# Pairwise field products: two stores split by partitions, ScalarE issuing the later stores, GpSimd giving TensorE's turns

## The chip, the cores and the metric

The kernel runs on one core of a Trainium2 chip. The metric is the device time of an execution in microseconds (us); the time before is the median of three runs. An execution's span, from its first to its last instruction, stands in the profile beside it.

## What is computed

The reference takes x of 4096 samples x 32 fields x 64 values, and a matrix W of 64 x 64, all float32:

```
vid = jnp.einsum('bfd,de->bfe', x, W)
idx_i, idx_j = jnp.triu_indices(32, k=1)
return x[:, idx_i, :] * vid[:, idx_j, :]
```

For each pair of fields i < j (496 pairs) the output is field i of x times field j of x times W, value by value. The output has 4096 x 496 x 64 float32 values, 520 MB; x has 33.6 MB.

## The kernel before

*Layout.* Two halves of the batch lie side by side in the 128 partitions (2 x 64 values), and the batch is cut into 16 tiles of 128 samples a half. One "field" of a tile is 128 partitions x 128 float32 values, 512 bytes a partition. `mem` in SBUF holds 446 such fields: inputs and products share it. On the HBM side a partition's fields lie one behind the other, in x as in the output, so that each DMA takes one contiguous run from each partition. The weights stand twice on the diagonal of a 128 x 128 matrix, so one matmul serves both halves.

*Work.* For each tile TensorE multiplies four fields at a time (line 237; 8 matmuls a tile) into `vid`, which fills PSUM. VectorE (line 173) makes the 496 products of a tile, many pairs an instruction, from `mem` and `vid` into `mem`. 68 stores ("slots") bring the products out, in the order in which they are made. `SLOTS` gives each store's number of fields and its place in `mem`; the places are reused again and again.

*Loads.* Tiles 0 to 5 are loaded at the start, by ScalarE's DMA queue. The other inputs come in two stretches of two loads each (128 and 32 fields): `LOAD_BEHIND = [24, 45]` says that SyncE issues them behind 24 and 45 stores. Stores are numbered from 0, so these are the places behind stores 23 and 44, of 128 fields each. Behind each stretch `held` makes the issuing engine wait, ahead of its next store, until the first matmul on the newly loaded tile (tile 6, tile 11) is done.

*Queues.* The class `Queue` wraps an issuing engine: `after_products(n)` waits until VectorE has done n instructions (line 133), `after(s)` waits for a DMA's semaphore to reach 16, each of them at most once. SyncE (`sp`) issues stores 0 to 65 (line 304) and the two stretches (line 198); ScalarE (`act`) issues the first loads and the last two stores. A DMA's semaphore gets 16 when all of it has landed.

*Turns.* TensorE waits for the semaphore `go` twice a tile (line 236 takes it back). ScalarE gives these turns: it waits until the half tile's fields have landed and VectorE has read the PSUM banks for the last time, and then increments `go`.

*The end.* ScalarE waits for all stores but the last and clears the semaphores; SyncE waits for the last store.

Of the kernel before, what the change touches and what calls it, by code (L numbers as in the profile page):

```python
# [12 lines left out]
P = 128  # L13
# [5 lines left out]
BANK = 4  # L19
# [33 lines left out]
LOAD_BEHIND = [24, 45]  # L53


SP_SLOTS = len(SLOTS) - 2

PAD = 24
PAD0 = 8
# [19 lines left out]
def products(at, ends):  # L79


    for kind, a, b, c, d in by_block():
        if kind == "row":
            rows, n, i0, di, j0, dj = c, d, b, 0, a, 1
        else:
            rows, n, i0, di, j0, dj = 16 // b, c, a, b, a + c + d, b
        r = k = 0
        while r < rows:
            room = ends[bisect_right(ends, at)] - at
            if k or room < n:  # L90
                m, w = 1, min(n - k, room)
            else:
                m, w = min(rows - r, room // n), n
            yield at, m, w, i0 + r * di + k, di, j0 + r * dj, dj
            at += m * w
            if k + w == n:
                r, k = r + m, 0
            else:
                k += w


HALF = F // 2


def fields(tiles, lo, n):

    return [(t, u - PLACE[t]) for u in range(lo, lo + n) for t in tiles if 0 <= u - PLACE[t] < F]
# [16 lines left out]
class Queue:  # L124
# [8 lines left out]
            self.engine.wait_ge(self.dve, n)  # L133
            self.products = n

    def after(self, s, known_to_product=None):

        if s.num not in self.seen and not (known_to_product and known_to_product <= self.products):
            self.engine.wait_ge(s, 16)
        self.seen.add(s.num)  # L140


# [33 lines left out]
def build(nc, x0, x, w, out):  # L176
    mem = nc.alloc_sbuf_tensor("mem", [P, UNITS, C], F32).ap()
    w2 = nc.alloc_sbuf_tensor("w2", [P, P], F32).ap()
    vid = nc.alloc_psum_tensor("vid", [P, F, C], F32).ap()

    go = nc.alloc_semaphore("go")
    pe = nc.alloc_semaphore("pe")
    dve = nc.alloc_semaphore("dve")
    sems = [go, pe, dve]

    def sem(name):
        sems.append(nc.alloc_semaphore(name))
        return sems[-1]

    track = Track()  # L190
    loaded = {}
    stored = []

    sp, act = Queue(nc.sync, dve), Queue(nc.scalar, dve)

    def load(q, dst, src, name, fields):
        s = sem(name)
        q.engine.dma_start(dst, src).then_inc(s, 16)
        for t, f in fields:
            loaded[t, f] = s  # L200
        return s


    a = PLACE[0]
    load(act, mem[:, a : a + HALF, :], x0[:, :HALF, :], "x0", [(0, f) for f in range(HALF)])
    ws = load(act, w2, w, "w", [])

    at = 0
    first_read = {}

    def stretch(q, tiles, runs, name):
        nonlocal at
        made = []
        for r, (lo, n) in enumerate(runs):
            q.after_products(track.reads(lo, lo + n))
            for k in track.stores(lo, lo + n):
                q.after(stored[k], first_read.get(k))
            made.append(load(q, mem[:, lo : lo + n, :], x[:, at : at + n, :], f"{name}{r}", fields(tiles, lo, n)))
            for u in range(lo, lo + n):
                track.store[u] = None  # L220
                track.read[u] = 0
            at += n
        return made

    held = stretch(act, *HEAD, "h")[-2], 16

    for tiles, first, step in WALKS:
        with nc.tensor.Fori(0, len(tiles)) as k:
            for b in range(F // BANK):
                if b % (HALF // BANK) == 0:
                    nc.tensor.wait_ge(go, 1)
                    nc.tensor.sem_inc(go, -1)  # L236
                nc.tensor.matmul(  # L237
                    vid[:, b * BANK : b * BANK + BANK, :],
                    lhsT=w2,
                    rhs=mem[:, bass.ds(k * step + (first + b * BANK), BANK), :],  # L240
                    start=True,
                    stop=True,
                ).then_inc(pe, 1)


    ends = sorted({*STARTS, *(STARTS[k] + c for k, cuts in CUTS.items() for c in cuts)})
    vector = Products(nc.vector, dve)
    done = 0
    bank_read = [0] * (F // BANK)
    dve_pe = dve_dve = 0  # L250
    slot = 0
    waiting = list(LOAD_BEHIND)
    stretches = list(STRETCHES)

    for t in range(NT):
        place = PLACE[t]
        for b in range(0, F // BANK, HALF // BANK):
            for s in [ws, *(loaded[t, f] for f in range(b * BANK, b * BANK + HALF))]:
                act.after(s)
            act.after_products(max(bank_read[b : b + HALF // BANK]))  # L260
            nc.scalar.sem_inc(go, 1)

        xt = mem[:, place : place + F, :]
        start = done
        for pos, m, n, i, di, j, dj in products(t * NP, ends):
            begin = STARTS[slot]
            size, lo = SLOTS[slot]
            u = lo + pos - begin
            o = mem[:, u : u + m * n, :]
            if m == 1:  # L270
                left = xt[:, i : i + n, :]
                right = vid[:, j : j + 1, :].to_broadcast([P, n, C])
            else:
                o = o.rearrange("p (m w) c -> p m w c", m=m)
                right = vid[:, j : j + (m - 1) * dj + 1 : dj, :].unsqueeze(2).to_broadcast([P, m, n, C])
                if di == 0:
                    left = xt[:, i : i + n, :].unsqueeze(1).to_broadcast([P, m, n, C])
                else:
                    left = xt.rearrange("p (m d) c -> p m d c", d=di)[:, i // di : i // di + m, i % di : i % di + n, :]
            waits = {}  # L280
            need = t * (F // BANK) + (j + (m - 1) * dj) // BANK + 1
            if need > dve_pe:
                waits[pe] = dve_pe = need
            for s in track.stores(u, u + m * n):
                if s not in first_read:
                    waits[stored[s]] = 16
                    first_read[s] = done + 1
            if track.reads(u, u + m * n) > dve_dve:
                waits[dve] = dve_dve = track.reads(u, u + m * n)

            vector.add(waits, done if t == 0 else start if t in FRESH else 0, o, left, right)
            done += 1
            for r in range(m):
                for f in range(i + r * di, i + r * di + n):
                    track.read[place + f] = done
                bank_read[(j + r * dj) // BANK] = done
            if pos + m * n == begin + size:
                if held is not None:
                    nc.sync.wait_ge(*held)
                    held = None  # L300
                q = sp if slot < SP_SLOTS else act
                q.after_products(done)
                s = sem(f"s{slot}")
                q.engine.dma_start(out[:, begin : begin + size, :], mem[:, lo : lo + size, :]).then_inc(s, 16)  # L304
                stored.append(s)
                for u in range(lo, lo + size):
                    track.store[u] = slot
                slot += 1
                if waiting and waiting[0] == slot:
                    waiting.pop(0)  # L310
                    tiles, runs = stretches.pop(0)
                    stretch(sp, tiles, runs, f"g{slot}_")
                    held = pe, tiles[0] * (F // BANK) + 1
    vector.emit()


    *landed, final = stored
    for k, s in enumerate(landed):
        act.after(s, first_read.get(k))
    numbers = sorted(s.num for s in sems)  # L320
    assert numbers == list(range(numbers[0], numbers[-1] + 1)) and final.num == numbers[-1]
    nc.scalar.sem_clear(range(numbers[0], numbers[-1]))
    nc.sync.wait_ge(final, 16)
    nc.sync.sem_inc(final, -16)
# [41 lines left out]
```

## Time and profile before

| what | value |
|---|---|
| median of three runs | 1284.24 us (1284.15 to 1284.56) |
| the profiled execution | 1284.14 us |
| its span | 1282.6 us |
| VectorE busy | 1080.3 us, 292 instructions |
| TensorE busy | 179.8 us, 256 matmuls |
| GpSimd busy | 0.2 us, 4 instructions |
| moved by DMA | 553.73 MB, mean 432 GB/s |
| HBM read, written | 33.62 MB, 520.09 MB |

A few marks for reading the lines below. PE is TensorE, DVE VectorE, POOL GpSimd; SPq and ACTq are the sequencers of SyncE and ScalarE, which issue DMAs; L173 is line 173 of the kernel. A line on a DMA queue gives packets, MB, and the time that the packets took as a share of the 16 DMA engines' time in the window asked for. A packet is listed in the window in which it starts, with its whole time, so that short windows can show shares over 100%. A line of waits gives the total in us, the number of waits and the longest. A line of the table of windows gives the window, its length, the busy time of PE, PEld, DVE and POOL (with counts), the granted clock, the DMA share, and GB/s. A line of the timeline or of the chain gives the start and the length in us.

### The profile page before, as it was taken

The page shows a single profiled execution, that of the slowest core. Times are in us where ns is not written, and L with a number is a line of the kernel's source. Part 1 is how long each engine was busy: PE and PEld are TensorE (multiplying, and loading weights), DVE is VectorE, ACT ScalarE, POOL GpSimd, SP SyncE. Part 2 cuts the span into 40 slices and gives each one's busy share as a digit, 9 for nine tenths or more (in the row PEclk, how much of TensorE's full clock was granted, in tenths as well). Part 3 has the DMA queues.
Part 4 walks back from the last instruction along what each step waited for, and adds up shares of the span by engine and source line. Part 5 has one row for each costly group of instructions (what it writes and reads, how often), then busy time and mean ns, then how long its engine had stood idle before and what let it go on. Part 6 is the DMA issues. An engine that isn't in the chain of part 4 may idle for free. (4 is left out here: it accounts for less than half of the span.)

```text
span 1282.6 us, 1142 instructions
## 1 busy us (share of the span) xinstructions
PE 179.8 (14%) x256; PEld 70.4 (5%) x256; DVE 1080.3 (84%) x292; POOL 0.2 (0%) x4
## 2 busy tenths in 40 slices
PE   3011040304010031012111201002212030111000
PEld 1000010101000010000000000001000010000000
DVE  5898999999996456989999998483898999899971
POOL 0000000000000000000000000000000000000000
PEclk7655565755565565565565656556557565565555
DMA  9999999999999999999999999999999999999999
GB/s 421 419 441 437 425 442 426 441 421 439 444 413 450 417 437 439 429 441 423 435 421 433 432 456 417 435 416 434 450 433 425 425 456 427 425 444 437 427 425 409
DMA packets 11090, 553.73 MB, mean 432 GB/s; under 512 B 1232, under 2 KB 1360, under 8 KB 1360
## 3 DMA queue, kind: packets, MB, share of 16 engines
q1 hardware_dynamic: 10080, 524.82, 94.7%
q10 hardware_dynamic: 1008, 28.90, 5.3%
q14 instruction: 2, 0.02, 0.0%
HBM read 33.62 MB, written 520.09 MB: 432 GB/s over the span
## 5 line engine op out<-in xcount | busy, mean ns | idle before, releaser
L173 DVE TENSOR_TENSOR mem<-mem,vid 128x1024 f32<-128x1024 f32 (+11 forms) x292 | 1080.3, 3770 | 174.8 <-DMA out_dram<-mem 144.4
L237 PE MATMUL vid<-mem,w 128*128 (+1 forms) x256 | 179.8, 870 | 1004.8 <-PEq L236 1004.8
L237 PEld LDWEIGHTS vid<-mem,w 128*128 128x128 f32 x256 | 70.4, 289 | 1113.4 <-issue 1113.4
L339 POOL MEMSET const-bfloat16-1.0<- 128x1 bf16 x1 | 0.1, 102 | 0.0
L339 POOL MEMSET const-uint8-127<- 128x1 uint8 x1 | 0.1, 102 | 0.0
L339 POOL MEMSET const-float32-0.0<- 128x1 f32 x1 | 0.1, 99 | 0.2 <-issue 0.2
L339 POOL MEMSET const-float32-1.0<- 128x1 f32 x1 | 0.1, 99 | 0.0
## 6 DMA issues: line engine op xcount, KB each, us to landing
out_dram<-mem SPq DMA_DIRECT2D x11, 7680.0 KB, 31.0
out_dram<-mem SPq DMA_DIRECT2D x11, 7168.0 KB, 23.1
out_dram<-mem SPq DMA_DIRECT2D x8, 6656.0 KB, 21.9
out_dram<-mem SPq DMA_DIRECT2D x4, 6144.0 KB, 24.2
out_dram<-mem SPq DMA_DIRECT2D x2, 5120.0 KB, 20.7
out_dram<-mem ACTq DMA_DIRECT2D x1, 7680.0 KB, 27.4
mem<-in_r_x_dram SPq DMA_DIRECT2D x2, 2048.0 KB, 60.5
out_dram<-mem SPq DMA_DIRECT2D x1, 3072.0 KB, 20.5
```

Source lines behind the costliest of these rows:

```text
L173: self.engine.tensor_tensor(*operands, MULT).then_inc(self.dve, 1)
L237: nc.tensor.matmul(vid[:, b * BANK : b * BANK + BANK, :], lhsT=w2, rhs=mem[:, bass.ds(k * step + (first + b * BANK), BANK), :], start=True ...
L339: nc = _bacc.Bacc("TRN2", target_bir_lowering=False, num_devices=1, dynamic_dma_scratch_size=256)
```

## The change

- Stores 23 and 44, the ones ahead of the two stretches of loads, are cut: 104 of the 128 fields go in one DMA of 128 partitions, and the last 24 fields in three DMAs, of partitions 0 to 111, 112 to 119 and 120 to 127. All four add to one semaphore, and whoever waits for the store waits for 64 instead of 16.
- Stores behind the second stretch (45 to 67) are issued by ScalarE, and so is the wait `held` ahead of them. Before, SyncE issued all but the last two.
- GpSimd gives TensorE's turns (`go`) instead of ScalarE.

```
-SP_SLOTS = len(SLOTS) - 2
+LATE = 24
+SPLIT = [0, 112, 120, 128]
...
-    sp, act = Queue(nc.sync, dve), Queue(nc.scalar, dve)
+    sp, act, gate = Queue(nc.sync, dve), Queue(nc.scalar, dve), Queue(nc.gpsimd, dve)
...
-                act.after(s)
-            act.after_products(max(bank_read[b : b + HALF // BANK]))
-            nc.scalar.sem_inc(go, 1)
+                gate.after(s)
+            gate.after_products(max(bank_read[b : b + HALF // BANK]))
+            nc.gpsimd.sem_inc(go, 1)
...
-                    waits[stored[s]] = 16
+                    waits.update([stored[s]])
...
+                q = sp if stretches else act
                 if held is not None:
-                    nc.sync.wait_ge(*held)
+                    q.engine.wait_ge(*held)
                     held = None
-                q = sp if slot < SP_SLOTS else act
                 q.after_products(done)
+                cut = size - LATE if slot + 1 in LOAD_BEHIND else size
+                parts = [(0, P, 0, cut)]
+                if cut < size:
+                    parts += [(p0, p1, cut, size) for p0, p1 in zip(SPLIT, SPLIT[1:])]
                 s = sem(f"s{slot}")
-                q.engine.dma_start(out[:, begin : begin + size, :], mem[:, lo : lo + size, :]).then_inc(s, 16)
-                stored.append(s)
+                for p0, p1, a, b in parts:
+                    q.engine.dma_start(
+                        out[p0:p1, begin + a : begin + b, :], mem[p0:p1, lo + a : lo + b, :]
+                    ).then_inc(s, 16)
+                stored.append((s, 16 * len(parts)))
```

More of the change, by code (lines that the diff above doesn't have):

```diff
@@ L134, in after_products, with after @@
             self.products = n
-    def after(self, s, known_to_product=None):
+    def after(self, s, n=16, known_to_product=None):
         if s.num not in self.seen and not (known_to_product and known_to_product <= self.products):
-            self.engine.wait_ge(s, 16)
+            self.engine.wait_ge(s, n)
         self.seen.add(s.num)
@@ L216, in stretch @@
             for k in track.stores(lo, lo + n):
-                q.after(stored[k], first_read.get(k))
+                q.after(*stored[k], first_read.get(k))
             made.append(load(q, mem[:, lo : lo + n, :], x[:, at : at + n, :], f"{name}{r}", fields(tiles, lo, n)))
@@ L314, in build @@
     vector.emit()
-    *landed, final = stored
-    for k, s in enumerate(landed):
-        act.after(s, first_read.get(k))
+    *landed, (final, _) = stored
+    for k, (s, n) in enumerate(landed):
+        act.after(s, n, first_read.get(k))
     numbers = sorted(s.num for s in sems)
```

## The prediction, made before the changed kernel was run

> **What bounds the kernel now.** I read the page's head first, then its DMA queues, then the waits, then single moments of the DMA list. The head, the DMA line and the queue part:
>
> ```profile
> span 1282.6 us, 1142 instructions
> PE 179.8 (14%) x256; PEld 70.4 (5%) x256; DVE 1080.3 (84%) x292; POOL 0.2 (0%) x4
> DMA  9999999999999999999999999999999999999999
> q1 hardware_dynamic: 10080, 524.82, 94.7%
> q10 hardware_dynamic: 1008, 28.90, 5.3%
> ```
>
> VectorE is the busiest compute engine, but the DMA line has a 9 in all 40 slices, and the two queues (q1 is fed by SyncE, q10 by ScalarE) take 94.7 + 5.3 = 100% of the 16 engines' span. Of VectorE's idle time, and of SyncE's, the waits say:
>
> ```profile
> DVE mem L173 <- DMA out_dram<-mem: 144.4, 31, 20.2
> DVE mem L173 <- PE vid L237: 30.3, 6, 11.5
> SPq L304 <- DVE mem L173: 1039.2, 62, 33.2
> SPq L198 <- DMA out_dram<-mem: 2.2, 2, 1.7
> ```
>
> VectorE waits 144.4 us for stores to free memory. SyncE waits for VectorE, yet this starves nothing, because a store once issued still stands in line. The table of windows shows the rate, and the summary of the stores (all instructions on the output) the time in line:
>
> ```profile
> 4.00:444.00 440.00, 68.31 (x96) 26.70 (x96) 388.89 (x105) 0.00 (x0) 0.58 1.00 434
> DMA to landing us min/median/max: 18.3/25.5/40.6
> ```
>
> The last column is GB/s. The queues move 524.82 + 28.90 = 553.72 MB, at 434 GB/s 1275.9 us. The span is 1282.6, so only 6.7 us of it are anything else: the start, the end, and what is lost at some moments. That is all a change of the transfers' order can win.
>
> Where is it lost? The DMA view of a short window lists the packets that start in it: their count, MB, and their time as a share of 16 engines in that window. So share x window = mean time of one round of 16 packets. Around the first stretch of loads (SyncE issues it behind store 23, and it moves about 447 to 472 us), one fence per window: 438.9 to 440 (middle of store 23), 443.9 to 445 (its last packets), 447.15 to 447.8 (first packets of the load, with 16 semaphore writes).
>
> ```profile
> q1 hardware_dynamic: 16, 1.05, 220.2%
> ```
> ```profile
> q1 hardware_dynamic: 16, 1.05, 285.1%
> ```
> ```profile
> q1 hardware_dynamic: 32, 1.05, 405.3%
> ```
>
> That is 2.202 x 1.1 = 2.422 us for a usual 65,536-byte packet, 2.851 x 1.1 = 3.136 us for the last of the store, 4.053 x 0.65 = 2.634 us for the first of the load. The change from store to load costs (3.136 - 2.422) + (2.634 - 2.422) = 0.93 us on every engine. The same before the second stretch, windows 841.6 to 842.6 and 844.6 to 845.4:
>
> ```profile
> q1 hardware_dynamic: 16, 1.05, 304.7%
> ```
> ```profile
> q1 hardware_dynamic: 32, 1.05, 323.0%
> ```
>
> 3.047 and 2.584 us: 0.62 + 0.16 = 0.79 us. Both together 1.72 us. From load back to store nothing is lost: 869.05 to 869.58, the first 57,344-byte packets of store 45:
>
> ```profile
> q1 hardware_dynamic: 32, 0.92, 400.9%
> ```
>
> 4.009 x 0.53 = 2.125 us for packet and semaphore write; 57,344/65,536 of 2.422 is 2.119.
>
> **The change, part by part.** The sum stands against the profiled execution, 1284.14 us (span 1282.6 and 1.5 around it); the median of the three runs is 1284.24, 0.1 above it.
>
> *Rows.* Stores 23 and 44 (128 fields each) become 104 fields for all 128 partitions, and 24 fields in three DMAs of 112, 8 and 8 partitions. No byte is added. In this trace a packet is one partition's row of a DMA: 128 rows give 16 engines 8 packets each, as the windows above show (16 equal packets at a time). A 24-field row is 12,288 bytes, 12,288/65,536 x 2.422 = 0.454 us. 112 rows are 7 for each of 16 engines. Where 8 rows go, no row here shows. Bounds: the two sets on different halves of the engines, 0; the same 8 engines twice, which then carry 9 rows instead of 8, +0.45 us a stretch, while the other 8 carry 7, -0.45; all on one engine, (7 + 16 - 8) x 0.454 = +6.8. I take the same eight: two DMAs of one shape go alike, as all the full ones do. **+0.91 us** for two stretches, on the half that sets the end.
>
> The Trainium skill's page "DMA: Bandwidth & Descriptors", section "Why a DMA increments its semaphore by 16 and not by 1", says that such a DMA uses the largest number of engines up to 16 that divides its outer size, and the lowest-numbered ones. By it 112 rows use 16 engines, and both sets of 8 the same first eight; the rows' term would be this +0.91 by the rule and 0 if the sets fell apart; no run here shows it.
>
> *More packets.* About 9 more data packets and 3 more semaphore writes on an engine a stretch. Small packets of the load, 470 to 471.6 us:
>
> ```profile
> q1 hardware_dynamic: 40, 0.66, 95.5%
> ```
>
> 0.955 x 1.6 x 16 / 40 = 0.611 us for 16,384 bytes; a quarter of 2.422 is 0.606. So 0.005 x 9 plus three writes under 0.01 each: at most 0.08 a stretch, **+0.1 us** in all.
>
> *The store-to-load loss.* Ends: none comes back (0), all comes back (-1.72). For the value I take engines that arrive late. Window 842.0 to 842.2, then 842.4 to 842.6, each hold one engine's last packet of store 44; the other 14 started before 841.95:
>
> ```profile
> q1 hardware_dynamic: 1, 0.07, 96.2%
> ```
> ```profile
> q1 hardware_dynamic: 1, 0.07, 81.0%
> ```
>
> 0.962 x 0.2 x 16 = 3.08 us and 0.81 x 0.2 x 16 = 2.59: the engine that is some 0.6 us late lost 0.17 against a mean of 0.62. The heavy half will come 0.9 us behind the light one, so it should lose some 0.45 less, and about 0.1 less on the load's first packet: **-1.1 us** over two stretches. The shorter packet in flight at the switch speaks for more, the light half's early reads for less.
>
> *The last engine.* The end is that of the slowest engine. Of the last semaphore writes, 1281.3 to 1281.65 and 1282.0 to 1282.2:
>
> ```profile
> q10 hardware_dynamic: 14, 0.00, 2.2%
> ```
> ```profile
> q10 hardware_dynamic: 1, 0.00, 0.3%
> ```
>
> One engine ends at least 0.35 us behind 14 others, at most 0.9. If it belongs to the light half the end comes earlier by about that, otherwise not. The halves' lead may be smaller by then, so I take less than the mean of the two: **-0.1**, ends -0.9 and 0.
>
> *Issues.* SyncE issues three DMAs more ahead of each stretch, 3 x 0.33 us:
>
> ```profile
> 408.16 0.33 SPq L304 DMA_DIRECT2D out_dram<-mem  x1
> 410.19 1.62 SPq L198 DMA_DIRECT2D mem<-in_r_x_dram  x2
> ```
> ```profile
> 809.43 0.33 SPq L304 DMA_DIRECT2D out_dram<-mem  x1
> 810.26 2.09 SPq L198 DMA_DIRECT2D mem<-in_r_x_dram  x2
> ```
>
> The first loads wait for a landed store until 410.19 anyway; the second ones go out some 0.5 us later. Their packets begin 34 us after the issue, at 844.6, behind stores in line; without that line it would cost 1.0 a stretch. So **0**. Semaphores of these two stores count to 64 instead of 16; VectorE's reuse waits see the same landing. Stores 45 to 67 go out from ScalarE with the same waits in the same order; behind them ScalarE has only the closing waits, and SyncE nothing but the last. The turns for TensorE, which would else stand behind these stores, move to GpSimd, which has 0.2 us of work.
>
> *The turn behind a load.* This is the one place with a thin cover. The chain, and ScalarE's first issue:
>
> ```profile
> 865.46 2.08 PE vid L237 x2
> 867.54 0.02 issue
> 867.56 0.34 SPq L304
> ```
> ```profile
> 0.72 0.38 ACTq L198 DMA_DIRECT2D mem<-in_r_x_dram  x1
> ```
>
> Store 45 is issued at 867.56, when the first matmul on the load is done. From issue to first packet takes 1.04 us (the DMA view has no packet up to 1.76 us and two at 1.76, after the issue at 0.72; the row is that of 0.5 to 1.77):
>
> ```profile
> q10 hardware_dynamic: 2, 0.02, 7.7%
> ```
>
> So its descriptors are there at about 868.60, and its first packet starts at 869.07 as the load ends: 0.47 us of cover. GpSimd's wait and increment aren't in the trace. Its only rows are four memsets like this:
>
> ```profile
> L339 POOL MEMSET const-float32-0.0<- 128x1 f32 x1 | 0.1, 99 | 0.2 <-issue 0.2
> ```
>
> Two such steps a turn would be 0.2 us; so I bound the turn at 0.2 us faster and 0.2 us slower than ScalarE's. I take **0**, covered by the 0.47. The light half may stand idle some tenths here, which its lead of 0.9 pays.
>
> Sum: +0.91 + 0.1 - 1.1 - 0.1 = -0.2: 1284.14 - 0.2 = 1283.9; with the median's 0.1, **1284.0 us**.
>
> **The rivals.**
>
> *No refund.* The heavy half carries its rows and loses as much at the switch as now: +0.91 + 0.1 = 1285.2 us. For it: the loss falls on all 16 engines, also on those a little late (3.08 us above). Against: the 2.59.
>
> *Full refund.* Small staggered packets switch from writing to reading without loss, and the sets fall on different halves, or the halves level out during the switch: -1.72 + 0.1 = 1282.5 us. For it: the loss is only in packets at the switch.
>
> *The turn comes late.* GpSimd answers a landed load so slowly that the DMA engines run dry: each stretch costs what the delay has above 0.47 us. It decides (0.2%, 2.6 us) from 0.47 + 1.3 = 1.8 us on; at 2.5 us it is 2 x 2.03 = +4.1, 1288.2 us. Against: landing to matmul now takes 0.4 us in all (the second load lands 54.8 us after its issue at 810.26):
>
> ```profile
> mem<-in_r_x_dram SPq DMA_DIRECT2D x1, 54.8
> ```
>
> *Each DMA pays a start of its own.* ScalarE's small load of the weights takes 4.8 us from issue to landing:
>
> ```profile
> w<-in_L_rec_W_dram ACTq DMA_DIRECT2D x1, 64.0 KB, 4.8
> ```
>
> If each of six more DMAs put even 2 us of that on the path, 1296 us. Against: the 434 GB/s above run over some two dozen DMAs in one queue. The same page of the Trainium skill, section "Anatomy of one DMA", gives a fixed 2.0 us a DMA, on another issuing path; it would make six DMAs 12 us; the trace disagrees for DMAs that stand in line.
>
> *One engine takes the eight rows twice:* +13.6 us, 1297.8. For it only that no row excludes it.
>
> **How the numbers follow.** Forecast (between 1283.2 and 1284.8) 0.55; no refund 0.17; full refund 0.17; late turn 0.05; a start for each 0.02; one engine 0.02; more than the whole loss saved 0.02 (1281.5 or less). From no change, 0.2% (2.6 us, 1281.7 to 1286.8) can be told. So faster 0.02 (the last case), slower 0.08 (0.04 of the late turn, whose other 0.01 stays within the bound, and 0.04 of the two dear ones), same 0.90. The range takes in both bounds of the switch and of the rows: 1282.4 to 1285.4; it leaves out the dear rivals and tails of the others.
>
> **What would show it.** In the changed trace: the last store packets before a load are 12,288 bytes and start in two groups some 0.9 us apart (rows right); packets at the switch sum to less than 0.93 and 0.79 us over their usual time (refund); store 45's first packet follows the load's last without a gap and stands on q10 (turn); the final semaphore writes come in one group rather than two (the halves level out). The prediction is wrong if the DMA share drops for over 1 us at 37% or 68% of the span, or if the final writes are spread over more than 2 us.

## The result, and the profile after

The changed kernel takes 1288.88 us (median of 6 runs, 1288.53 to 1289.11); the kernel before, run beside it, 1284.2. The ratio is 1.0035, 95% interval 1.0024 to 1.0045: slower by 4.7 us. The prediction had said 1284.0, within 1282.4 to 1285.4, and was wrong.

The head and the DMA lines of the changed kernel's profile:

```profile
span 1287.6 us, 1148 instructions
DMA  9999999999999999999999999999999999999999
DMA packets 11410, 553.74 MB, mean 430 GB/s; under 512 B 1296, under 2 KB 1424, under 8 KB 1424
```

The span grew by 5.0 us. The bytes (553.74 MB against 553.73) and the full DMA line are as before. So either the same bytes took longer *in their packets*, while the DMA engines still look busy, or the engines stood idle too briefly for the line. The page's slices, 32 us each, can't show which; the landing times of the loads show where. The DMA view of a short window lists the issues in it with the time to landing, in us, as the last number. First load of the first stretch before (issued at 410.19) and after (412.06), first load of the second stretch after (816.16):

```profile
mem<-in_r_x_dram SPq DMA_DIRECT2D x1, 57.6
```
```profile
mem<-in_r_x_dram SPq DMA_DIRECT2D x1, 58.3
```
```profile
mem<-in_r_x_dram SPq DMA_DIRECT2D x1, 54.2
```

Landed: 410.19 + 57.6 = 467.8 before, 412.06 + 58.3 = 470.4 after, +2.6. The second: 810.26 + 54.8 = 865.1 before, 816.16 + 54.2 = 870.4 after, +5.3. So each stretch adds about 2.6 us, and the two together are the whole loss.

Inside the switch, packets that start in 443.5 to 447 (93 of the last 24 fields, and a semaphore write), then 447.14 to 447.2 (two packets):

```profile
q1 hardware_dynamic: 94, 1.14, 99.5%
```
```profile
q1 hardware_dynamic: 2, 0.02, 426.4%
```

0.995 x 3.5 x 16 / 93 = 0.60 us a packet, and 4.264 x 0.06 x 16 / 2 = 2.05 us for those two; the price in the prediction was 0.454. Not all of the difference comes from the cut: over all 128 packets of the last 24 fields the mean is 0.65 us in this trace, and 0.55 where one DMA of all rows brings them to the same switch (`SPLIT = [0, 128]`, below). Then the table of windows, 472 to 473.6 (GB/s last, the DMA share before it), and the chain there:

```profile
472.00:473.60 1.60, 1.60 (x3) 0.57 (x3) 0.00 (x0) 0.00 (x0) 0.50 0.48 205
```
```profile
470.38 0.04 POOLq L264
...
470.73 2.08 PE vid L240 x2
...
472.83 19.32 DMA out_dram<-mem
```

At 205 GB/s about half of the engines stand dry, while the others still finish their loads: store 24 goes out only at 472.83 (before: 470.23), after the first matmul, which needs the load from the *slowest* engine. (The trace counts two instructions for each matmul of the program, 256 for 16 tiles of 8, hence "x2".) GpSimd itself is quick: landed at 470.35, matmul at 470.73.

### The profile page after: what moved, and what is told of

Its sections match the earlier page's. It is cut to its first block, busy times and chain, and to the rows that moved or that the text cites. A ratio compares the mean times of both kernels' runs of the same rounds, so it can differ in the third digit from the quotient of the medians.

```text
span 1287.6 us, 1148 instructions
## 1 busy us (share of the span) xinstructions
PE 182.3 (14%) x256; PEld 71.0 (6%) x256; DVE 1080.4 (84%) x292; POOL 0.2 (0%) x4
## 2 busy tenths in 40 slices
DMA packets 11410, 553.74 MB, mean 430 GB/s; under 512 B 1296, under 2 KB 1424, under 8 KB 1424
## 4 chain that ended last, share of the span: by engine, by line
DVE 34%; DMA 24%; another core or an unknown queue 16%; issue 1%; PE 1%; ACTq 0%; POOLq 0%; DVEq 0%
DVE mem L175 34%; DMA out_dram<-mem 24%; PE vid L240 1%; ACTq L312 0%; POOLq L264 0%; DVEq L173 0%
```

## The experiments

Each is a copy of the kernel before or of the changed one, with the edit shown. "Before" beside them took 1284.1 to 1284.3 us.

**The parts of the change, one at a time.** The cut alone:

```
-                q = sp if stretches else act
+                q = sp if slot < SP_SLOTS else act
...
-            nc.gpsimd.sem_inc(go, 1)
+            nc.scalar.sem_inc(go, 1)
```

> The cut of stores 23 and 44 alone; SyncE issues stores 0 to 65 and ScalarE gives the turns, as before. The changed kernel took +4.7 us. Theory A (crowding: the rows of the sets 112-119 and 120-127 lie behind few ports of SBUF, so that the engines that carry such a set share them; seen as 12,288-byte packets of 1.2 to 2.1 us where 0.46 is usual): all of it is here, 1288 to 1289.5. Theory B (the turns by GpSimd and the stores by ScalarE come late; SyncE issued store 24 at 472.83 instead of 470.23): 1284 to 1285.2, the row skew at most.

Measured 1289.54 us, ratio 1.0040 (1.0026 to 1.0055). The queues alone:

```
-                cut = size - LATE if slot + 1 in LOAD_BEHIND else size
+                cut = size
```

> ScalarE issues the stores behind the second stretch, GpSimd gives the turns, no store is cut. Theory A (crowded ports): 1284.2 within 0.6. Theory B (late turns and issues): 1288 to 1289.

Measured 1284.0, ratio 0.9997 (0.9988 to 1.0007). The whole loss is in the cut; who issues stores and who gives turns makes no difference that can be measured.

**Small packets, without other partitions.** `SPLIT = [0, 128]`, so the last 24 fields go in one DMA of all rows:

> Stores 23 and 44 as 104 fields and 24 fields, both of all 128 partitions, queues as before. Small packets at the switch, without a skew and with each engine on rows of its own. Theory A (crowded ports): 1283.3 to 1284.5. Theory C (it is the small packets ahead of a load that lose, each of them): 1287 to 1289. The prediction's idea that a shorter packet at the switch gets part of the 1.7 us back would show as 1282.5 to 1283.8.

Measured 1284.58, ratio 1.0002 (0.9992 to 1.0012). Small packets ahead of a load lose nothing that can be told, and get nothing back (1284.58 lies just above theory A's 1284.5).

**Halves against even and odd.** Both cut the 24 fields into two DMAs of 64 rows, 4 rows an engine each; they differ in which partitions go together:

```
 halves:        SPLIT = [0, 64, 128]
 even and odd:  SPLIT = [(0, 128, 2), (1, 128, 2)]   # first, end, step
```

> The last 24 fields by partitions 0-63 and 64-127: two DMAs that give each of 16 engines 4 rows, no skew, 8 packets of 12,288 bytes an engine as in the version of all rows. The Trainium skill's page SBUF - State Buffer, section Door 1, says that partitions 0-63 reach 8 of the 16 ports. Theory A (crowded ports): two engines share a port all through, 8 x 0.454 us become 8 x 0.91, +3.6 us a stretch, 1288 to 1291.5. Theory C (small packets) and theory D (skew of the halves, which then wait for the slowest at the load): as the version of all rows, 1283.3 to 1284.7.

> The last 24 fields of stores 23 and 44 by the even and the odd partitions: like the version of halves two DMAs of 64 rows, 4 rows an engine each, no skew, 8 packets of 12,288 bytes; only which partitions are read together differs, and here each DMA reaches all 16 ports. Theory A (crowded ports): engines still meet on a port, but can step apart; 1285 to 1289.5, at least 2.5 us under the halves (1292.2). If 64 rows in a DMA cost by themselves, whatever the partitions: 1291.5 to 1293.

Halves: 1292.22, ratio 1.0061 (1.0044 to 1.0078). Even and odd: 1284.77, ratio 1.0005 (0.9995 to 1.0015). The contrast is that of theory A, but both lie outside its ranges: halves 0.7 us above 1291.5, even and odd 0.2 us below 1285, with no loss that can be told. The table of windows, 443.2 to 445.2, for halves, even and odd, and all rows in turn:

```profile
443.20:445.20 2.00, 0.00 (x0) 0.00 (x0) 0.00 (x0) 0.00 (x0) 0.50 1.02 233
```
```profile
443.20:445.20 2.00, 0.00 (x0) 0.00 (x0) 0.07 (x1) 0.00 (x0) 0.50 1.06 449
```
```profile
443.20:445.20 2.00, 0.00 (x0) 0.00 (x0) 0.24 (x1) 0.00 (x0) 0.50 1.00 424
```

All three have a DMA share of 1.0, but halves move 233 GB/s and the others 449 and 424. Of the packets that start in 444.2 to 445.2, again for halves, even and odd (11 of the 46 are semaphore writes), and all rows:

```profile
q1 hardware_dynamic: 18, 0.22, 107.5%
```
```profile
q1 hardware_dynamic: 46, 0.43, 101.7%
```
```profile
q1 hardware_dynamic: 32, 0.39, 92.7%
```

1.075 x 1 x 16 / 18 = 0.96 us a packet with halves, 0.46 with the other two: a factor of two. Halves and even and odd have the same rows a DMA, the same packets and no skew: only the partitions differ, by 7.5 us. This is the clearest pair of the study. The Trainium skill's page "SBUF — State Buffer", section "Door 1: The DMA port swizzle", says that partitions 0 to 63 reach only 8 of SBUF's 16 DMA ports, and so half the rate; the trace agrees, with 233 against 424 GB/s. What the pair shows is that the choice of partitions sets the time of a packet. In every run a row of the output in HBM goes with its partition, so no run here tells SBUF's side of a DMA from HBM's; that the ports are the reason rests on the page and on the factor of two. Why even and odd partitions lose nothing, where the expectation still had engines meet on a port, is open.

**The same cut far from a load.** `if slot in [18, 34]` instead of the stores ahead of the loads, once with 112, 8 and 8 partitions, once with 112 and 16, once with all rows:

> The same cut of 112, 8 and 8 partitions, but at stores 18 and 34 (128 fields each), with no load near; stores 23 and 44 whole; queues as before. Theory A (crowded ports): the small packets are slow here too, the last engine lands some 2.5 us behind the first behind each of these stores, 1286 to 1289.5 (less where the next change to a load levels the engines again). Theory E (it takes the change from store to load to make the small packets slow): 1284.2 to 1285.2, packets of 0.46 us.

> Partitions 0-111 and 112-127 (7 rows and 1 row an engine, no skew) at stores 18 and 34, far from a load. With 112, 8 and 8 there it was +10.6 us. If crossings of the 112 rows make most of it, +6 to +9, 1290 to 1293.5; if the two sets of 8 and the skew do, +2 to +5, 1286.2 to 1289.3.

> Stores 18 and 34 as 104 and 24 fields of all 128 partitions, far from a load. The control for the same place with 112, 8 and 8 partitions (+10.6 us). Theory A (crowded ports): 1284.0 to 1284.8, every 12,288-byte packet 0.46 us. If two more DMAs or small packets cost by themselves: 1286 and more.

Measured 1294.87 (1.0083, 1.0067 to 1.0100), 1291.76 (1.0058, 1.0041 to 1.0075) and 1284.65 (1.0002, 0.9992 to 1.0012). The packets that start in 349.5 to 352, with 112, 8 and 8, then with all rows, and one packet that starts at 352.39 to 352.40 in the first of them:

```profile
q1 hardware_dynamic: 70, 0.86, 99.1%
```
```profile
q1 hardware_dynamic: 84, 1.03, 97.6%
```
```profile
q1 hardware_dynamic: 1, 0.01, 2078.8%
```

0.991 x 2.5 x 16 / 70 = 0.57 us a packet against 0.976 x 2.5 x 16 / 84 = 0.46; and one 12,288-byte packet of 20.788 x 0.01 x 16 = 3.33 us, seven times its usual time. No load is needed for the loss; the first of the three even lies 5.4 us above the expected 1286 to 1289.5. The 112 rows and 16 rows, without a skew, make 7.6 of the 10.6 us, which is more than the sets of 8 with their skew. The long packets seem to share with more than their own set: while that one ran, three 61,440-byte packets of the next store, started at 352.50, 352.72 and 352.88 on other engines, took 3.6 to 3.7 us, and most later ones 2.27.

**112 and 16 ahead of the loads.** `SPLIT = [0, 112, 128]`:

> The last 24 fields by partitions 0-111 and 112-127: both give all 16 engines the same number of rows (7 and 1), so no skew. Theory A (crowded ports): the 16 engines' rows 112-127 stand behind a quarter of the ports, 4 x 0.454 us where one would do, +1.4 us a stretch, and the first part's rows cross too: 1286 to 1289. Theory D (what costs is the skew of 9 rows against 7): 1284 to 1284.8.

Measured 1287.72, ratio 1.0028 (1.0017 to 1.0039): 3.5 us slower with 8 rows on each engine. Skew is not what most of the loss comes from; it and the two sets of 8 add 1.8 us (1289.54 against 1287.72). The traces, of one execution each, say how: the 128 packets of the first cut take 0.66 us on average in both, but the 16 engines' parts of the first load behind them land within 1.4 us with 112 and 16, and within 2.8 us with 112, 8 and 8. The sets of 8 lay the same packet time on fewer engines, and the slowest one counts.

**Twice the bytes in the same DMAs.** `LATE = 48`, with the cut alone:

> The cut alone with the last 48 fields instead of 24 in the three DMAs: twice the bytes in the same number of DMAs and packets. Theory A (crowded ports): the loss goes with the bytes, +8.5 to +11.5, 1293 to 1296. If it is a price for each DMA or each packet: +5.2 and the skew's other 0.9, 1289.5 to 1290.8.

Measured 1295.01, ratio 1.0081 (1.0064 to 1.0098): +10.7 us where 24 fields cost +5.3. The loss goes with the bytes in these DMAs, not with the number of DMAs or packets.

**Blocks against combs.** Same sizes, counts and skew; the sets of 8 rows differ:

```
 blocks: LATE = 12, SPLIT = [(0, 96), (96, 104), (104, 112), (112, 120), (120, 128)]
 combs:  LATE = 12, SPLIT = [(0, 96), (96, 128, 4), (97, 128, 4), (98, 128, 4), (99, 128, 4)]
```

> The last 12 fields (6,144 bytes a row) of stores 23 and 44 by partitions 0-95 and four blocks 96-103, 104-111, 112-119, 120-127. Rows on an engine 10 against 6, so the bytes' skew is the changed kernel's (2 rows of 6,144 for 1 of 12,288, +-0.45 us). Theory A (crowded ports): each block stands behind 2 ports for 8 engines, 0.91 instead of 0.23 us each, up to 4 x 0.68 + 0.45 = 3.2 us a stretch, less where the engines spread over two blocks at a time: 1286.5 to 1290.5. Theory D (skew alone): as the changed kernel, 1287.5 to 1289.5, and the same as the version with combs.

> As the version of four blocks, but each set of 8 takes every fourth partition of 96 to 127 (96, 100, ... 124, then 97, 101, ...): same sizes, same counts, same skew; only the partitions differ, and each set has 8 ports for 8 engines. Theory A (crowded ports): only the skew (+0.45 us a stretch) and crossings in the first part are left, 1284.2 to 1286, and at least 1.5 us under the version of blocks. Theory D (skew alone): the same time as the blocks, within 0.5.

Blocks 1289.2 (1288.37 to 1291.98; ratio 1.0029 to 1.0062), combs 1287.94 (1287.23 to 1288.22; 1.0017 to 1.0039). The sign is that of crowded ports, but 1.3 us is less than the 1.5 expected, the intervals overlap, the combs lie 1.9 us above their range, and both times lie in the range of theory D, skew alone, though further apart than its 0.5. As a test of the sets the times are inconclusive. Both versions share the part of 96 rows: its packets that start in 445.2 to 447 move at 222 GB/s with blocks and at 225 with combs, the same half rate. The sets themselves do differ in the traces: of the last 32 packets to start at the first cut, three take 0.9 to 1.1 us with blocks, and none over 0.47 with combs, where 0.23 is the usual time.

**Without the wait for the matmul.** The hold ahead of stores 24 and 45 taken out, of the kernel before and of the cut alone:

```
-                    held = pe, tiles[0] * (F // BANK) + 1
```

> The kernel before without the wait for the first matmul on the new tile ahead of stores 24 and 45 (only the wait at the start stays). The DMA queue is full there anyway, so both theories: 1283.8 to 1284.8. It is the base for the next one.

> The cut alone, without that wait. With it the engines that were ready early stood idle for up to 1.8 us until the slowest had landed the load. Theory F (the slowest engine's own delay sets the end, the idle time of the others costs nothing): 1288.2 to 1290, the semaphores of the last stores spread over 3 us and more. Theory G (the wait turns the spread into a loss for all engines; left alone, the late engines catch up at the next change from store to load and in the end only part is left): 1285.5 to 1287.8.

Measured 1285.07 (1.0005, 0.9996 to 1.0015; 0.3 us above its range) and 1288.71 (1.0033, 1.0020 to 1.0046). The cut costs 3.6 us without the hold, 5.3 with it. So the slow engines' own delay is most of the loss (theory F's time), and the idle time of the others, which the hold turns into a loss for all, about 1.6 us, if the two differences are exact; by the intervals each is uncertain by about 2 us, so that share is an indication, not shown. That the engines no longer wait is plain: 472 to 473.6 without the hold,

```profile
472.00:473.60 1.60, 1.60 (x3) 0.61 (x2) 0.00 (x0) 0.00 (x0) 0.50 1.24 512
```

against 205 GB/s above. The spread at the end, expected to be over 3 us, was smaller: the last 16 semaphore writes start between 1284.8 and 1286.6, and without cut and hold they lie nearly as far apart, 1281.7 to 1283.4. So theory F has its time but not its second sign. The spread did exist on the way, 2.9 us at the first load behind the first cut and 3.4 behind the second, and shrank over the following 400 us.

## Why the prediction was wrong, point by point

- *What bounds the kernel* held: DMA engines full from end to end, so that a slower packet on the slowest engine goes straight into the time.
- *Rows* is the step that failed. It counted rows for each engine and priced each at 12,288/65,536 of a usual packet, 0.454 us. That a row takes this time whatever partitions its DMA covers was never argued; every DMA in the trace before has all 128 rows, so no row of it showed another case. In the changed trace the packets took 0.60 us on average in the rows shown, and the two at 447.14 to 447.2 took 2.05. What took its place: the time of a packet depends on which partitions are read together, shown by halves against even and odd (0.96 against 0.46 us); that several engines then meet on one SBUF port is the reading of it. The cut cost +5.3 us where the term had +0.91. The count itself was right. That the sets of 8 use 8 engines each is borne out: 4-byte semaphore writes grew from 1232 to 1296, 64 = 2 x (16 + 8 + 8). That it is the same eight can be read in the trace of the cut far from a load: there eight packets of the first set each end where a semaphore write and then a packet of the second set start (one ends at 355.72, and the next starts there), so that eight engines carry 9 rows and eight carry 7.
- *The store-to-load loss*, -1.1 us, did not come. With small packets of all rows the time is 1284.58, nothing gained. Their trace shows the loss still there: 0.548 us a packet ahead of the first load against 0.463 far from one, 8 x 0.085 = 0.68 us an engine, and 0.61 at the second; the kernel before lost 0.71 and 0.62 on its last store packets. That a late engine lost less in one switch was one packet's row, and it didn't carry a saving.
- *The turn behind a load* had the right size for GpSimd (470.35 to 470.73, 0.38 us; 0.4 before), and the queues alone were rightly 0. But the cover of 0.47 us was worked out for a load that lands on all engines at about the same time, and that the light half's "lead of 0.9 pays" for idle tenths was wrong: half of the engines stood dry at 205 GB/s, and the next stretch began from the slowest. The share of 0.48 over 1.6 us, at 37% of the span, is the prediction's own sign of being wrong. It adds some 1.6 us by the last pair, if that pair is taken as exact.
- *More packets*, +0.1, is not contradicted: 1.0002 for all rows at both places.
- *Issues*, 0, stands although the size was off: four DMAs took not 4 x 0.33 but 4.20 us to issue,

```profile
407.81 4.20 SPq L312 DMA_DIRECT2D out_dram<-mem  x4
```

  under stores that were still in line for 35 us.
- *The last engine*, -0.1, can't be told: 15 of the 16 last semaphore writes now fall in 1286.6 to 1287.0,

```profile
q10 hardware_dynamic: 15, 0.00, 2.1%
```

  and the last one starts at 1287.1. So a straggler is still there, 0.2 us behind the others here, 0.5 in the trace of the cut alone and 0.3 before.

None of the rivals named the mechanism. The late turn of GpSimd has nearly the measured time, 1288.2 us, but by chance: the queues alone lost nothing, and its turn took 0.38 us. "One engine takes the eight rows twice" was nearest: many bytes through one narrow place, but it looked for it in the engine and not in the partitions. The chance of 0.08 for slower was too low because the unknown price of a new DMA shape was bounded only by how its rows are counted, not by how long one takes.

Open are: which rows an engine takes and how many engines share what in the 112 rows, whether it is SBUF's side or HBM's that they share, and why the same cut costs twice as much far from loads. No version tried here beats the kernel before.

## What to carry to other kernels

In these runs a DMA over all 128 partitions kept its rate (424 GB/s at the switch), and a cut by partition ranges did not (233 with 0 to 63 and 64 to 127, 356 with 0 to 111 and 112 to 127), though the DMA share still read 100%. Look at GB/s and at the time of a packet beside its bytes, not at the share. Cut by columns (1284.58 for the same fields) or by a stride over all partitions (1284.77) if a store must be cut; and where a wait needs a whole load, the slowest engine's delay becomes everyone's.

## What the runs showed of the hardware

- A 12,288-byte packet took 0.46 us in a DMA of all rows and, far from a load, up to 3.33 us where 8 engines each took one of 8 neighbouring partitions. By the Trainium skill's page "SBUF — State Buffer", section "Door 1: The DMA port swizzle", such a block lies on 2 ports, so four engines a port would make 4 x 0.46 = 1.8 us, an estimate from that page and the 0.46. The measurement is above it, and packets of the next store were drawn out from 2.27 to 3.7 us meanwhile, so more than these four seem to have shared something.
- An engine stays late for long in the stream of stores: behind the first cut far from a load the 16 engines' parts of a DMA landed 5.2 us apart at 376 us and still 5.1 us apart at 478 us; behind the hold, 1.1. Without the hold the spread shrank slowly, from 3.4 to 1.9 us in 400 us. Two cuts far from loads cost 10.6 us, two ahead of loads 5.3; why isn't shown.
- Cutting by even and odd partitions was as fast as not cutting by rows: 449 against 424 GB/s at the switch, 1284.77 against 1284.58 us.
- The change from store to load cost the same with packets of 12,288 as of 65,536 bytes: 0.68 and 0.61 us an engine against 0.71 and 0.62.
